# A four-layer convolution and scan kernel: loads in another order, image 0 without the previous image's convolution, setup in two parts, and VectorE in the first and last image

## The chip, the cores and the metric

The kernel runs on one core of a Trainium2 chip. A core has a matrix engine (TensorE; PE in the profile, PEld for its weight loads), a vector engine (VectorE, DVE), an engine for activations (ScalarE, ACT), a general one (GpSimd, POOL), and one that here only issues transfers (SyncE, SP). Each takes its instructions in the order of its own queue and waits on semaphores for the others. Transfers between DRAM and the on-chip memory (SBUF) run on DMA engines beside all this; any of SP and ACT can issue them. The metric is device time in microseconds of one execution, as the median over several.

## The reference

Sixteen images of 192 channels and 32 × 32 pixels (L = 1024) go through four residual layers, each behind a group norm. All is fp32.

```python
x = x + L0(gn(x))   # mLSTM block + silu branch -> 3x3 convolution -> batch norm over all images -> leaky relu
x = x + L1(gn(x))   # channel attention: q, k, v by 1x1 and depthwise 3x3, softmax; project, depthwise, project
x = x + L2(gn(x))   # selective scan in four directions over L: Gelu(depthwise 3x3(in_proj)), project, scan, norm, gate
x = x + L3(gn(x))   # sum of shifted copies (8 shifts in y, 7 in x), weighted by softmax of tanh(products); 1x1, Gelu
```

What matters here: layer 0's batch norm needs statistics of all sixteen images, so everything after it waits for the last image's convolution. L1 and L2 hold ten depthwise 3 × 3 convolutions per image, counted in blocks of 96 or 128 channels: two for v, three for q and k, two for the second one, three in L2. Each output is a sum of nine shifted inputs, each with a factor per channel. L2's recurrence is h[t] = dA[t]·h[t−1] + xt[t].

## The kernel before, in words

Two parts run one after the other.

**Layer 0** is `layer0` (L153). It loads its weights and small vectors, nearly all from the SP queue in the order of the text, and makes two products of weights on PE (`ps<-wg,wT`, `ps<-v_ln_b,w_up` at L39), so that the gates and the norm's offset need no work of their own per image. Then `tc.For_i` at L386 runs over the sixteen images. In pass b a generator `conv3` gives the 3 × 3 convolution of image b − 1, piece by piece: 60 pieces of two matrix passes, in which the function `fill(n)` takes n pieces wherever PE would wait for other engines. Fifteen pieces come before the part of the pass that is written out by hand, two or three each in it. In pass 0 the previous image is taken modulo sixteen, and what is convolved is the padded map `ypad`, which is still zero; what it writes is overwritten by the last convolution, which stands by itself after the loop. Each convolution leaves its result in `ydram` and its statistics in `sdram`.

**Layers 1 to 3** are `LayersB.run` (L860). `setup` (L884) folds the statistics into a scale and an offset (`bsc`, `bsh`), and makes what the layers need: for each depthwise convolution nine diagonal matrices of its factors, made on DVE (L948) and stored to DRAM (`dqd`, `dvd`); the product `w1d` of two weights on PE; the scan's constants (`A`, `dskip`, `xpj`, `sel`), the permutations of L3 (`perm`). All its loads and stores stand in SP's queue, ahead of those of image 0.

Then image by image: `prepare(b)` does L1 and the first half of L2, `scans` the recurrence, `complete(b)` the rest of L2, and L3. These two are generators too; each `yield` names the engine of the next piece. During the scans of image b the pieces of `complete(b-1)` and `prepare(b+1)` are put into gaps by a planner with a cost per instruction and engine clocks of its own (`fits`, `advance`). `prepare(0)` has no scans to lie beside and runs through before them, `complete(15)` after them. In these the order is that of dependences.

In `prepare`, `fill(i, p, pairs)` multiplies by a 1 × 1 weight and copies into a padded map `pad`; `taps` loads the nine diagonals in three thirds into three buffers `dg`; `conv` runs, for each half of the map, nine matrix passes over shifted views of `pad`. The helper's line is L766 in the profile for all engines. At the end a Gelu gives `xg`, which is stored in `xxd` and loaded back by `fetch_xx` into `xx`, since `xx` of the image before may still be read; then the other half of L2's input, z, is made on PE, goes through Gelu on ACT and is stored in `zd`. `begin` starts the first scans: it projects `xx`, makes the steps, stores them (`dld`, `dud`) and loads them back, each row copied to sixteen states (`dl`, `du`).

The scans are 192 units per image, of 128 × 1024 each: ACT makes dA (L1801) and copies du to xt (L1797), DVE multiplies xt by B (L1808) and scans (L1817), POOL multiplies by C (L1829), PE sums over states (L1859). SP loads dl, du and the states in the same order throughout.

In `complete`, each half of the map is loaded from `yd`, normed, gated by z from `zd`, multiplied out and added to x; POOL makes the products. Then fifteen shifted products of x per channel block are made by POOL into a ring of buffers `t`, go through tanh on ACT, and are summed by PE, with symmetric shifts used twice (nine series of two blocks, 34 instructions). The softmax and the weighted sum follow, by blocks, and the last 1 × 1 product `fin`.

Of the kernel before, what the change touches and what calls it, by code (L numbers as in the profile page):

```python
# [20 lines left out]
L = H * W  # L21
HL = L // 2
P6 = 96
# [129 lines left out]
def layer0(tc, cx, NB, ydram, sdram):  # L153
    nc, I = cx.nc, cx.I
    with ExitStack() as ctx:
# [15 lines left out]
        def vec(name, p):  # L171
            v = I[name]
            t = wp.tile([p, v.shape[0] // p], F32, name="v_" + name)
            nc.sync.dma_start(t, v.rearrange("(a p) -> p a", p=p))
            return t
# [5 lines left out]
        w_q = wp.tile([128, 3, INNER], F32, name="w_q")  # L181
        nc.scalar.dma_start(w_q, I["w_q"].rearrange("(k p) o -> p k o", p=128))
        w_k = wp.tile([128, 3, INNER], F32, name="w_k")
        nc.scalar.dma_start(w_k, I["w_k"].rearrange("(k p) o -> p k o", p=128))
# [3 lines left out]
        w_down = wp.tile([128, 3, 256], F32, name="w_down")  # L188
        w_lin = wp.tile([P6, 2, 256], F32, name="w_lin")
        for t, nm, p in ((w_down, "w_down", 128), (w_lin, "w_lin", P6)):  # L190
            nc.sync.dma_start(t[:, :, 0:C], I[nm].rearrange("(k p) o -> p k o", p=p))
            nc.sync.dma_start(t[:, :, C:], I[nm][:, 128:C].rearrange("(k p) o -> p k o", p=p))
        w_c2 = wp.tile([128, 9, C], F32, name="w_c2")
        nc.sync.dma_start(w_c2, I["conv2_wT"][0:128])
        w_c2p = wp.tile([128, 2, 3, C], F32, name="w_c2p")
        for u in range(2):
            r = slice(64 * u, 64 * u + 64)
            taps = I["conv2_wT"][128:C].rearrange("p (y x) o -> p y x o", x=3)
            nc.sync.dma_start(w_c2p[r, 0], taps[:, :, u, :])
            nc.sync.dma_start(w_c2p[r, 1], taps[:, :, 2, :])  # L200
        ln_w, ln_b = vec("ln_w", P6), vec("ln_b", P6)
        b_up = vec("b_up", 128)
        conv_b, skip = vec("conv_b", 128), vec("skip", 128)
        mh_w, mh_b = vec("mh_w", 128), vec("mh_b", 128)

        def vec3(name):
            t = wp.tile([128, 2], F32, name="v_" + name)
            v = I[name].rearrange("(p o) -> p o", o=1)
            nc.sync.dma_start(t[:, 0:1], v[0:128])
            for u in range(2):  # L210
                nc.sync.dma_start(t[64 * u : 64 * u + 64, 1:2], v[128:C])
            return t

        b_down, b_lin, c2_b = vec3("b_down"), vec3("b_lin"), vec3("conv2_b")


        b_if = []
        for nm in ("b_i", "b_f"):
            t = wp.tile([128, 1], F32, name="v_" + nm)
            nc.vector.memset(t, 0.0)  # L220
            for r in range(4):
                for u in range(2):
                    nc.sync.dma_start(
                        t[32 * r + NH * u : 32 * r + NH * u + NH, :], I[nm].rearrange("(h o) -> h o", o=1)
                    )
            b_if.append(t)
        b_i, b_f = b_if
        conv_k = wp.tile([128, 3, 4], F32, name="conv_k")
        nc.sync.dma_start(conv_k, I["conv_k"].rearrange("(k p) t -> p k t", p=128))
        mask = wp.tile([128, 2 * CH], BF16, name="mask")  # L230
        identb = wp.tile([128, 128], BF16, name="identb")
        hmask = wp.tile([128, 4 * HW1], F32, name="hmask")
        nc.sync.dma_start(hmask, I["c_hmask"])
# [8 lines left out]
        for r in range(4):  # L242
            nc.sync.dma_start(sel[32 * r : 32 * r + NH], I["c_sel"])
# [48 lines left out]
        with tc.tile_pool(name="a_pre", bufs=1) as pre:  # L292
            m32 = pre.tile([128, CH], F32, name="m32")
            nc.sync.dma_start(m32, I["c_causal"])
            nc.vector.tensor_copy(
                mask.rearrange("p (i t) -> p i t", i=2),
                m32.unsqueeze(1).to_broadcast([128, 2, CH]),
            )
            wg = pre.tile([128, 9, 2 * NH], F32, name="wg")
            nc.sync.dma_start(wg[:, :, 0:NH], I["w_i"].rearrange("(k p) h -> p k h", p=128))  # L300
            nc.sync.dma_start(wg[:, :, NH:], I["w_f"].rearrange("(k p) h -> p k h", p=128))
            nc.vector.tensor_copy(wg_v[:, :, 0 : 2 * NH], wg[:, 6:9, :])
            for i, nm in enumerate(("w_qT", "w_kT")):
                wT = pre.tile([128, 3, INNER], F32, tag="wT%d" % i, name="wT")
                nc.sync.dma_start(wT, I[nm].rearrange("(k p) o -> p k o", p=128))
                for m in range(3):
                    p = ps()[:, 0 : 2 * NH]
                    matmuls(
                        nc, p,
                        [(wT[:, j, m * 128 : (m + 1) * 128], wg[:, 3 * i + j, :]) for j in range(3)],  # L310
                    )
                    o = wg_qk[:, m, 0 : 2 * NH]
                    if i == 0:
                        nc.vector.tensor_copy(o, p)
                    else:
                        nc.vector.tensor_add(o, o, p)

            p = ps()
            for m in range(6):
                matmuls(  # L320
                    nc, p[:, m : m + 1],
                    [(w_up[:, a, m * 128 : (m + 1) * 128], ln_b[:, a : a + 1]) for a in range(2)],
                )
            nc.vector.tensor_add(b_up, b_up, p[:, 0:6])
            for a in range(2):
                nc.vector.tensor_scalar(
                    w_up[:, a, :], w_up[:, a, :], ln_w[:, a : a + 1], None, op0=ALU.mult
                )

        x_in = wp.tile([128, 3, L + 3], F32, name="x_in")  # L330
# [55 lines left out]
        with tc.For_i(0, NB, 1) as b:  # L386
# [158 lines left out]

            conv = conv3((b + NB - 1) % NB)
# [173 lines left out]

        for _ in conv3(NB - 1):
            pass
# [86 lines left out]
class LayersB:  # L809
# [5 lines left out]
    def __init__(self, tc, cx, NB, ydram, sdram, out):  # L815
        self.tc, self.cx, self.NB = tc, cx, NB
        self.nc, self.I = cx.nc, cx.I
        self.ydram, self.sdram, self.out = ydram, sdram, out
# [35 lines left out]
    def run(self):  # L854
        tc, NB = self.tc, self.NB
        self.bank, self.turn = None, 0
        with ExitStack() as ctx:
# [12 lines left out]
            for _ in self.prepare(0):  # L870
                pass
            self.fetch_xx()
            self.begin()
# [10 lines left out]
    def setup(self):  # L884
        tc, nc, cx, wp, I, NB = self.tc, self.nc, self.cx, self.wp, self.I, self.NB
# [3 lines left out]
        self.w1d = dp.tile([P6, 2, C], F32, name="w1d")  # L889
# [41 lines left out]
        with tc.tile_pool(name="b_pre1", bufs=2) as pre:  # L931
            taps = []
            for m in range(3):
                t = pre.tile([128, 9], F32, tag="tq%d" % m, name="tq")
                with nc.allow_non_contiguous_dma("taps by channel"):
                    nc.sync.dma_start(t, I["dw_qkT"][:, m * 128 : (m + 1) * 128].rearrange("t c -> c t"))
                taps.append((128, t, self.dqd[m]))
            t = pre.tile([128, 3, 9], F32, tag="tw", name="tw")
            nc.sync.dma_start(t, I["dw_w"].rearrange("(g p) t -> p g t", p=128))
            taps += [(128, t[:, g, :], self.dqd[3 + g]) for g in range(3)]  # L940
            for i, nm in enumerate(("dw_v", "dw_kv")):
                t = pre.tile([P6, 2, 9], F32, tag="tv%d" % i, name="tv")
                nc.sync.dma_start(t, I[nm].rearrange("(a p) t -> p a t", p=P6))
                for a in range(2):
                    taps.append((P6, t[:, a, :], self.dvd[i, a]))
            for n, t, dst in taps:
                d = pre.tile([n, 9, n], F32, tag="diag", name="diag")
                nc.vector.tensor_mul(  # L948
                    d, cx.ident[0:n, 0:n].unsqueeze(1).to_broadcast([n, 9, n]),
                    t.unsqueeze(2).to_broadcast([n, 9, n]),  # L950
                )
                nc.sync.dma_start(dst, d)
            wpj = pre.tile([P6, 2, C], F32, tag="wpj", name="wpj")
            nc.sync.dma_start(wpj, I["w_proj"].rearrange("(a p) o -> p a o", p=P6))
            wkv = pre.tile([P6, 2, C], F32, tag="wkv", name="wkv")
            nc.sync.dma_start(wkv, I["w_kvT"].rearrange("(a p) o -> p a o", p=P6))
            w1 = pre.tile([P6, 2, C], F32, tag="w1", name="w1")
            for a in range(2):
                p = self.mm()[0:P6, 0:C]
                matmuls(nc, p, [(wpj[:, i, a * P6 : (a + 1) * P6], wkv[:, i, :]) for i in range(2)])  # L960
                nc.vector.tensor_copy(w1[:, a, :], p)
            nc.sync.dma_start(self.w1d, w1)
# [1005 lines left out]
```

## Time and profile before

The time is 15763.65 us, the median of three executions (15760.87 to 15764.36). The profiled execution took 15761.82 us, and its span, from the first to the last instruction, is 15760.0 us.

| part of the span | us |
|---|---|
| startup, to the loop over images | 0 to 58 |
| sixteen images of layer 0, 201.6 us each | 58 to 3282 |
| last convolution alone | 3282 to 3328 |
| setup, and the load and norm of image 0 | 3328 to 3388 |
| `prepare(0)` | 3388 to 3628 |
| projection and steps for the first scans | 3628 to 3668 |
| scans of sixteen images | 3668 to 15583 |
| `complete(15)` | 15583 to 15760 |

In the whole span PE is busy 80%, DVE 78%, POOL 63%, ACT 59%; DMA moves 154 GB/s on average. These are means over stages with different limits. A row of the trace gives start, length, engine, line, operation, what is written and read, shape and count; in brackets stands how long the engine had been idle before it, and whose work ended that.

### The profile page before, as it was taken

The numbers are of one execution on the slowest core, as the hardware profiler recorded it, in microseconds if no ns is written. First come the engines' busy times: TensorE is split into PE (matmuls) and PEld (weight loads), VectorE is DVE, ScalarE is ACT, GpSimd is POOL, SyncE is SP. The second block draws the span as 40 slices with busy tenths as digits, with TensorE's granted clock in tenths as the row PEclk, the third lists the DMA queues.
The fourth block names the chain that finished last, engine by engine and source line by source line (L and its number), as shares of the span: only waits on it lengthen the run. The fifth ranks groups of instructions, "written<-read, shape, count | busy, mean of one in ns | idle before, by whom it ended". The sixth has DMA issues, their size and how long they took to land. (4 is left out here: it accounts for less than half of the span.)

```text
span 15760.0 us, 197355 instructions
## 1 busy us (share of the span) xinstructions
PE 12662.9 (80%) x72684; PEld 5062.6 (32%) x72684; DVE 12218.0 (78%) x10138; ACT 9273.8 (59%) x12098; POOL 9921.9 (63%) x5837
## 2 busy tenths in 40 slices
PE   8999999987777878778777777777787777878755
PEld 4555555542222222222222222222222222222212
DVE  4444444416898989989888898988989898988995
ACT  3333333325666666666666666666666666666664
POOL 0000000005687878787878787878878787878886
PEclk9999999998787878878788888888888887878766
DMA  1000000016787877778787878787877777777774
GB/s 26 15 15 15 15 14 15 15 47 168 193 202 196 198 199 192 207 185 209 180 209 182 210 186 209 185 210 186 204 193 196 194 200 192 198 201 188 203 181 114
DMA packets 858797, 2421.52 MB, mean 154 GB/s; under 512 B 117952, under 2 KB 237840, under 8 KB 850192
## 3 DMA queue, kind: packets, MB, share of 16 engines
q1 hardware_dynamic: 848592, 2407.09, 59.7%
q8 instruction: 583, 9.55, 0.3%
q10 hardware_dynamic: 9280, 2.08, 0.1%
q14 instruction: 342, 2.80, 0.1%
HBM read 2025.36 MB, written 366.67 MB: 152 GB/s over the span
## 5 line engine op out<-in xcount | busy, mean ns | idle before, releaser
L1829 POOL TENSOR_TENSOR hc<-h,cb 128x1024 f32<-128x1024 f32 x3072 | 7245.4, 2371 | 2057.6 <-DVE h L1817 1546.5
L1817 DVE TENSOR_TENSOR_SCAN h<-dA,xt 128x1024 f32<-128x1024 f32 x3072 | 6914.9, 2273 | 303.6 <-POOL hc L1829 295.9
L1808 DVE TENSOR_TENSOR xt<-xt,bb 128x1024 f32<-128x1024 f32 x3072 | 3632.9, 1227 | 929.7 <-ACT xt L1797 800.6
L1801 ACT ACTIVATE dA<-dl,A 128x1024 f32<-128x1024 f32 x3072 | 3506.3, 1146 | 778.6 <-DMA dl<-dld 670.2
L1859 PE MATMUL acc<-hc,sel 128*32 128x256 f32 x24576 | 2399.7, 471 | 1756.8 <-POOL hc L1829 1753.8
L766 PE MATMUL mm<-pad,dg 96*96 96x512 f32 (+1 forms) x5760 | 2964.3, 650 | 14.4 <-ACT pad L766 11.0
L1797 ACT COPY xt<-du 128x1024 f32<-128x1024 f32 x1536 | 1557.7, 1014 | 1387.9 <-DVE h L1817 1216.3
L1859 PEld LDWEIGHTS acc<-hc,sel 128*32 128x32 f32 x24576 | 560.6, 120 | 4094.9 <-POOL hc L1829 2956.9
L766 PEld LDWEIGHTS mm<-pad,dg 96*96 96x96 f32 (+1 forms) x5760 | 1022.0, 191 | 1517.1 <-issue 1400.8
L583 POOL TENSOR_TENSOR vw<-va,gtok 128x396 f32<-128x396 f32 x112 | 95.3, 851 | 1707.1 <-ACT va L575 1707.1
L766 PE MATMUL mm<-x,wgt 96*128 96x512 f32 (+1 forms) x1664 | 1055.2, 770 | 114.9 <-ACT z L766 42.8
L766 POOL TENSOR_TENSOR t<-x 96x512 f32<-96x512 f32 (+7 forms) x544 | 689.6, 1290 | 212.5 <-PE mm L766 199.9
L1850 PE MATMUL acc<-y,ident 128*128 128x512 f32 x576 | 444.1, 863 | 452.1 <-ACT y L1869 451.4
L678 POOL TENSOR_TENSOR x_in<-x_in,sz 128x384 f32<-128x384 f32 x128 | 116.8, 913 | 749.8 <-DVE x_in L674 674.0
L766 POOL TENSOR_TENSOR dlh<-dlh,e 128x512 f32<-128x512 f32 x384 | 488.6, 1272 | 157.4 <-ACT e L766 151.4
L766 PE MATMUL mm<-d,xT 128*96 128x256 f32 x2048 | 562.3, 412 | 19.2 <-ACT o L766 17.4
L766 POOL TENSOR_TENSOR duh<-dlh,xx 128x512 f32<-128x512 f32 x384 | 537.4, 1399 | 30.2
L766 PE MATMUL mm<-xd,dtw 12*128 12x512 f32 x768 | 532.8, 779 | 14.1 <-ACT dlh L766 14.1
L766 PEld LDWEIGHTS mm<-x,wgt 96*128 96x128 f32 (+1 forms) x1664 | 338.1, 223 | 633.5 <-issue 360.9
L374 PE MATMUL pc<-ypad,w_c 128*128 128x512 f32 (+1 forms) x1224 | 468.3, 631 | 89.3 <-PEq L386 46.1
L609 DVE TENSOR_TENSOR D<-D,s 128x256 f32<-128x256 f32 x768 | 271.0, 415 | 325.9 <-ACT D L606 325.9
L606 ACT ACTIVATE D<-s 128x256 f32<-128x256 f32 x768 | 232.7, 390 | 430.6 <-PE s L600 430.6
(314 smaller groups left out, 15277.6 us busy)
## 6 DMA issues: line engine op xcount, KB each, us to landing
dl<-dld SPq DMA_DIRECT2D x1536, 512.0 KB
du<-dud SPq DMA_DIRECT2D x1536, 512.0 KB
dld<-dlh SPq DMA_DIRECT2D x384, 256.0 KB
dud<-duh SPq DMA_DIRECT2D x384, 256.0 KB
bb<-xdr SPq DMA_DIRECT2D x128, 512.0 KB
cb<-xdr SPq DMA_DIRECT2D x128, 512.0 KB
dg<-dqd SPq DMA_DIRECT2D x288, 192.0 KB
xxd<-xg SPq DMA_DIRECT2D x16, 1536.0 KB
```

Of the source, the lines that this page charges most:

```text
L374: nc.tensor.matmul(p[r, :], lhsT=w_, rhs=v, start=(n == 0), stop=(n == 14))
L606: nc.scalar.activation(d, S[j][:, two], AF.Exp)
L609: nc.vector.tensor_mul(d, d, S[j][:, 2 * CH :])
L678: nc.gpsimd.tensor_mul(hT[:, :, cs], hT[:, :, cs], sz[:, :, cs])
L766: return f(out, *args, **kw)
L1797: self.nc.scalar.copy(self.xt[n], self.du[n])
L1801: self.nc.scalar.activation(self.dA[u % 3], self.dl[n % 2], AF.Exp, scale=self.A[:, blk, n : n + 1])
L1808: self.nc.vector.tensor_mul(self.xt[(n + 1 + blk) % 2], self.xt[n % 2], self.bb[blk])
L1817: nc.vector.tensor_tensor_scan(*views, 0.0, op0=ALU.mult, op1=ALU.add)
L1829: self.nc.gpsimd.tensor_mul(*views)
L1850: nc.tensor.matmul(acc, lhsT=self.cx.ident, rhs=self.y[:, g, half(pair)], start=True, stop=False)
L1859: nc.tensor.matmul(self.acc[rows4(q), q4(s)], lhsT=self.sel[:, m, :], rhs=self.hc[u % 3][:, q4(q)], start=False, stop=(s + m + blk == 3),)
```

## The change

**Startup.** The weights that the two products need (`w_qT`, `w_kT`, `w_i`, `w_f`, `w_up`) are loaded ahead of those that the loop needs (`w_q`, `w_k`, `w_down`, `w_lin`, `w_c2`, `w_c2p`); the loads are shared between SP's queue and ACT's. The product `w1d` of setup is made here. The pool of the temporary tiles is closed after it, and the loop's weights are loaded then.

**Image 0.** The body of the loop becomes a function `image(b, conv)`. Image 0 is called with an empty iterator in place of the convolution, and the loop runs from 1 to 15.

**Setup.** It is cut in two: `setup` keeps what `prepare(0)` needs, `setup_scans` the rest, and is called after twenty pieces of `prepare(0)`. The diagonals are no longer made in `setup`. In image 0, `taps` loads the nine factors per channel (`tv`), DVE makes the diagonals right in `dg`, and SP stores them from there for the later images. `conv` in image 0 gives PE only the first half of the map; the second is made by DVE, with one `tensor_scalar` and eight `scalar_tensor_tensor` on shifted views of `pad`.

**End of `prepare(0)`.** Gelu writes to `xx` itself, with no store and load; `begin` comes ahead of the pieces of z.

**Last image.** `complete(15)` loads y by channel group into `xx` and z into `dA`, both at its beginning, instead of by halves; its products are made by DVE in place of POOL. As a result, the first loads of y lie inside the last image's scans.

```diff
         nc.scalar.dma_start(w_up, I["w_up"].rearrange("(a p) o -> p a o", p=P6))
-        w_q = wp.tile([128, 3, INNER], F32, name="w_q")
-        nc.scalar.dma_start(w_q, I["w_q"].rearrange("(k p) o -> p k o", p=128))
...
+        for i, nm in enumerate(("w_qT", "w_kT")):
+            wTs.append(prp.tile([128, 3, INNER], F32, tag="wT%d" % i, name="wT"))
+            nc.scalar.dma_start(wTs[i], I[nm].rearrange("(k p) o -> p k o", p=128))
...
+        nc.scalar.dma_start(w1d, w1)
+        pre.close()
+
+        w_q = wp.tile([128, 3, INNER], F32, name="w_q")
+        nc.sync.dma_start(w_q, I["w_q"].rearrange("(k p) o -> p k o", p=128))
...
-        with tc.For_i(0, NB, 1) as b:
+        def image(b, conv):
...
-            conv = conv3((b + NB - 1) % NB)
...
+        image(0, iter(()))
+        with tc.For_i(1, NB, 1) as b:
+            image(b, conv3(b - 1))
...
-            for _ in self.prepare(0):
+            first = self.prepare(0)
+            for _ in range(20):
+                next(first)
+            self.setup_scans()
+            while not self.parked:
+                next(first)
+            self.begin()
+            for _ in first:
                 pass
-            self.fetch_xx()
-            self.begin()
...
+    def taps(self, p, src, w, first):
         d = [self.slot("dg", [p, 3, p], "dg", 3) for _ in range(3)]
+        tv = None
+        if first:
+            tv = self.sm.tile([p, 9], F32, tag="tv", name="tv")
+            self.nc.sync.dma_start(tv, w)
         for t in range(3):
+            three = slice(3 * t, 3 * t + 3)
+            if first:
+                self.nc.vector.tensor_mul(
+                    d[t], self.cx.ident[0:p, 0:p].unsqueeze(1).to_broadcast([p, 3, p]),
+                    tv[:, three].unsqueeze(2).to_broadcast([p, 3, p]),
+                )
+                self.nc.sync.dma_start(src[:, three, :], d[t])
+            else:
+                self.nc.sync.dma_start(d[t], src[:, three, :])
+        return d, tv
...
+    def conv(self, out, i, p, taps):
         for hf in range(2):
+            if hf and tv is not None:
+                yield "DVE", 0
+                o = rows(out[:, half(hf)])
+                for t in range(9):
+                    v = self.pads[i][0:p, 16 + t // 3 : 32 + t // 3, t % 3 : t % 3 + W]
+                    if t == 0:
+                        nc.vector.tensor_scalar(o, v, tv[:, 0:1], None, op0=ALU.mult)
+                    else:
+                        nc.vector.scalar_tensor_tensor(
+                            o, v, tv[:, t : t + 1], o, op0=ALU.mult, op1=ALU.add
+                        )
+                continue
...
+        xx = xg if b else self.xx
         for g in range(3):
-            nc.scalar.activation(xg[:, g, :], xg[:, g, :], AF.Gelu, bias=self.dw2b[:, g : g + 1])
+            nc.scalar.activation(xx[:, g, :], xg[:, g, :], AF.Gelu, bias=self.dw2b[:, g : g + 1])
...
+        products = nc.vector if last else nc.gpsimd
+        if last:
+            for g in range(3):
+                nc.sync.dma_start(self.dA[g], self.zd[b, g])
+                nc.sync.dma_start(self.xx[:, g, :], self.yd[g])
...
-                    nc.gpsimd.tensor_mul(t[:, o:], xa[:, o:], xa[:, : L - o])
-                    nc.gpsimd.tensor_mul(t[:, :o], xa[:, :o], xa[:, L - o :])
+                    products.tensor_mul(t[:, o:], xa[:, o:], xa[:, : L - o])
+                    products.tensor_mul(t[:, :o], xa[:, :o], xa[:, L - o :])
```

## The prediction

> **What bounds the kernel now.** I read the busy time by stretch first, with borders that I set where the trace changes character: startup, image loop, last convolution, setup, first image's preparation, its projection, scans, and the last image's end in three pieces. Columns are length, busy time of PE, PEld, DVE, ACT and POOL with counts, the granted TensorE clock, DMA share, GB/s.
>
> ```profile
> 0.00:58.00 58.00, 12.80 (x60) 12.80 (x61) 7.33 (x41) 1.28 (x1) 6.00 (x11) 1.00 0.46 108
> 58.00:3282.00 3224.00, 3104.27 (x28977) 1689.50 (x28977) 1420.86 (x2849) 1249.30 (x2383) 290.90 (x480) 0.99 0.05 14
> ...
> 3328.00:3388.00 60.00, 4.15 (x13) 3.23 (x14) 25.45 (x60) 13.65 (x20) 6.70 (x4) 0.53 0.62 153
> 3388.00:3628.00 240.00, 228.72 (x582) 100.78 (x581) 9.27 (x24) 50.97 (x89) 0.21 (x1) 0.96 0.16 47
> ...
> 3668.00:15583.00 11915.00, 9151.28 (x42504) 3186.22 (x42504) 10739.57 (x7134) 7877.75 (x9500) 9526.45 (x5244) 0.80 0.77 196
> ```
>
> Scans are three quarters of the span and the change leaves them alone. It works in the other stretches: in startup and setup no engine is busy, so something is waited for; preparation is PE alone (228.72 of 240) with DVE idle. Then I read single instructions in order of time, with the wait ahead of each in brackets.
>
> ```profile
> 45.20 4.04 PE L39 MATMUL ps<-wg,wT 128*128 128x24 f32 x18 [45.20 <-DMA wT<-in_w_qT]
> ...
> 3365.30 0.33 SPq L1119 DMA_DIRECT2D x<-in_x  x1
> ...
> 3373.00 1.24 ACT L766 ACTIVATE y<-y,bsh,bsc 96x1024 f32<-96x1024 f32 x1 [7.02 <-DMA y<-ydram]
> ...
> 3431.39 15.62 PE L766 MATMUL mm<-pad,dg 128*128 128x512 f32 x36
> ...
> 3632.93 8.00 PE L766 MATMUL mm<-xx,xpj 128*108 128x512 f32 x12 [4.83 <-DMA xx<-xxd]
> ...
> 15592.03 4.36 PE L766 MATMUL mm<-yh,on 128*128 128x512 f32 x6 [9.79 <-DMA yh<-yd]
> ...
> 15649.39 42.47 POOL L766 TENSOR_TENSOR t<-x 96x1024 f32<-96x1024 f32 x34 [12.50 <-ACT x L766]
> ```
>
> PE does nothing until a weight lands at 45.20; image 0 of the second part starts when its own load, issued at 3365.30 behind some 50 others, has landed; each depthwise convolution costs PE 15.62; a round trip through DRAM, then a POOL series, set the end.
>
> **Startup, about −31.** The transposed weights and gates go ahead of w_q, w_k and the convolution weights. Some 2.7 MB stand up to and including them; DMA moved 237 to 361 GB/s between 3 and 17 us of the trace, so at 270 they take 10 us and land at 13 to 15. Then PE works 4.04 + 5.26 + 4.01 = 13.3 as now, and 2.85 more for the product of w_proj and w_kvT that setup makes now: 14 + 16.2 = 30 for the first group matmul (L91), which is at 61.83 now. Behind that product stand w_q, w_k, w_down and the rest, on SP after its small loads and after a free completion slot; w_q is needed only about 40 us after the group matmul, so this is covered unless SP is over 20 us late. Range −22 to −33.
>
> Here a rule speaks against the change: the Trainium skill ("DMA: Bandwidth & Descriptors", Issuing engines are not separate DMA queues) says that DMAs of all queues share the same 16 engines and that a second issuing engine saves only issue time, usually small. Were it small, all 6.28 MB of the first 60 us would have landed by 6.28/270 = 23 us, and reordering would be worth 8. The trace disagrees: from 20 to 34 us almost nothing moves (0 to 33 GB/s), as SP issues small loads one behind another. I take the trace: −31.
>
> **No convolution in image 0, about −20.** Its 120 matmul passes take about 43 us of PE, on an empty map. But many fill waits. Those between 58 and 80 (14.9 us) stand in the norms' waits for DVE and ACT: worth 1.3 to 3. In the written-out schedule from 141.6 to 242 it is 28.3: five groups of about 2.6 and eight of 1.9. Next to each stand ACT and DVE steps of 1.2 to 1.4 per chunk that PE waits for anyway, so I take 1.7 and 1.0 of each: 16.5. One loop edge goes (46.1 us idle ahead of L374 over 15 edges, 3.1), but image 0 must drain into the loop: 0 to 3. Ends 10 and 43; −20, near the low end because the schedule puts these pieces into waits.
>
> **Setup in two parts, about −27.** About 14 loads stand before x instead of 50, so x is issued when the norm's coefficients are there, near 3337.5, not 3365.30: −27.8. DVE's small constants of the second part (dskip, bn3) now fall between the norm's steps: +0.7. The diagonals go to the convolutions.
>
> **Preparation of image 0, about −87.** PE keeps one half of each of ten convolutions, 18 passes = 7.72; DVE makes the other while PE works. DVE's price: one scaling and eight multiply-adds of 512. The multiply-add in the trace is
>
> ```profile
> L422 DVE SCALAR_TENSOR_TENSOR xact<-x_in,conv_k,xact 128x1024 f32<-128x1024 f32 x144 | 177.5, 1278 | 0.6
> L418 DVE TENSOR_SCALAR xact<-x_in,conv_k 128x1024 f32<-128x1024 f32 x48 | 34.6, 748 | 0.6
> ```
>
> and TENSOR_TENSOR takes 658 for 512 against 1218 for 1024, so 512 less costs 560: 1278 − 560 = 0.72, and about 0.45 for the scaling: 0.45 + 8 × 0.72 = 6.2, plus three diagonal thirds (0.4 to 0.5) of the next: 7.6. PE's own share per convolution is fill 3.43 + 7.72 = 11.1, so DVE fits. By convolution: two of v 2 × 7.72 = 15.4; three of q/k 3 × 7.72 less about 0.7 each, because PE takes the transposes of DVE's half first: 21; two kv, which stand back to back, 31.07 to about 16.4: 14.7; three of the last projection 23.2 less 0.6: 22.6. Sum 73.7. The Gelu writes xx itself, no store and load: PE starts the projection at 3632.93 now, and Gelu ended at 3619.6: −13.2. That is 86.9.
>
> A second rule is against this. The Trainium skill ("Vector Engine (DVE) Microarchitecture Reference", Points that are easy to get wrong) has it that a multiply-add of that form with two SBUF sources that aren't bf16 runs at half throughput. By that each would cost 0.72 + 0.53 = 1.25, DVE's half 10.5 and 11.8 with diagonals: longer than PE's 11.1; each q/k convolution would wait about 2.8 more, the kv pair 7, the last projection about 5 in all; −24 of the gain is lost (total 176). L422 has exactly two fp32 SBUF sources and its 1278 is 60 ns over the plain product's 1218. I take L422.
>
> **Projection to scans, +1.5 (−6 to +6).** The z work used to be hidden in the round trip: three Gelus with two table loads (1.28) each and six copies (0.54). It now stands on ACT between the first decays, and behind ACT wait the copies xt for DVE (L1808): about 3. SP's z stores and the next image's loads wait in order for those Gelus, with the first dl and du loads near them. Against it PE comes to the projection without a pause (its 12 passes take 0.67 each there, 0.43 in the convolutions): −2; and du is issued ahead of a store: −2 or so.
>
> **Inside the scans, +2 (0 to 6).** The order on all engines is the same in all 3072 units. Only in the last image SP takes two loads xx<-yd that must wait for the store of yd to land (3 to 5 us each); dl and du loads stand behind them, and their two-deep rings cover most of it.
>
> **Tail, about −40 (30 to 45).** Now two halves run one after the other: load, means, product, with POOL products 1.24 each (3.71 for three), from 15587.78 to x added at 15642.4. After, y and z are already there except for the last group; the first subtraction is at about 15592.9 instead of 15596.4, the second half needs no load (15615.09 to PE at 15619.40 now) and overlaps; 2 × 6 products at 0.66 instead of 1.24 save the rest: −20. Then 18 rolled products: 16 in two pieces, DVE 1218 plus 98 for the second, 2 at 1.22: 23.5, against 42.47 on POOL: −19. ACT's tanh, 1.06 each, and PE's sums, 1.08 at a clock of 0.50, run beside it and are next in line: they would set 19 to 20. Two adds at the end: −1.2.
>
> **Sum.** −31 −20 −27 −87 +1.5 +2 −40 = −201.5, say −200. The profiled execution took 15761.82 with a span of 15760.0; the span becomes 15560 and its execution 15562. The median is 1.8 above that execution: 15563.6, say 15563.
>
> **Rivals.** (1) DVE doesn't hide: pad reads, diagonals and slots stand one behind another on it, PE waits 2.5 more for each convolution: 25 less, 15588. For: DVE takes diagonals in order and each must wait for PE to leave its slot. Against: 7.6 of 11.1. (2) Given back in the queue: SP's in-order stores and waits late at the start of the scans and in the last image cost 15, w_q comes 15 late in startup, less in between: 15600. For: ACT waits 667.3 us for dl and DVE 800.6 for xt in the scans, so no slack. Against: rings. (3) More: most of image 0's 43 us goes, PE stays at full clock in projection: 15535. (4) The change does nothing that can be measured: the waits it removes are only moved to the next load. Against: PE's 73.7 us cannot return as a load. (5) Slower: landing of dl worsens in all units, because buffers in DRAM and on chip are laid out anew. It needs (200 + 31)/3072 = 0.075 us per unit, a third of the 0.217 that ACT waits for dl now; at 0.09 the time is 15840. Against: same loads in the same order, and h takes 2239 to 2290 ns whatever its buffer.
>
> **Chances.** Differences under 0.2% (31.5 us) can't be told from none here. Forecast as summed 0.58; (1) 0.14; (2) 0.12; (3) 0.11; (4) 0.02; (5) 0.03. So faster 0.95, same 0.02, slower 0.03. The range: parts' ends (22–33, 10–43, ±1, 60–95, ±6, 0–6, 30–45) combined as independent give 15540 to 15600 or so; to take in (1), (2) and (3) it is 15525 to 15625.
>
> **What would show it.** First matmul near 14 and first group matmul near 30; first image's pass 20 shorter than the 201.6 of others; y's ACTIVATE 8 us after the coefficients; 18 passes per convolution with DVE multiply-adds of 0.72 beside; no xxd for image 0; scans again 11915 long; DVE rolls near 24. Wrong if DVE's multiply-adds take over 1 us, if the scan stretch moves by over 15, or if PE still waits for a weight at 40.

## The result, and the profile after

The changed kernel takes 15604.58 us, the median of four executions (15591.93 to 15608.56), against 15764.01 (15760.87 to 15766.58) for the kernel before on the same chip: 0.9897 of the time, with an interval of 0.9886 to 0.9909. That is 159.4 us less, where 200 were forecast. The profiled execution took 15591.93 us and its span is 15590.1, 169.9 below the span of before.

First the busy time of two stretches of the kernel after, with borders at the same events as before (columns: length; busy time and count of PE, PEld, DVE, ACT, POOL; granted clock, DMA share, GB/s): the sixteen images of layer 0, and the first image's preparation.

```profile
29.00:3283.00 3254.00, 3111.09 (x28865) 1693.29 (x28865) 1419.54 (x2847) 1248.00 (x2380) 290.84 (x480) 0.98 0.05 14
...
3341.00:3495.00 154.00, 124.34 (x340) 57.39 (x341) 76.62 (x145) 42.23 (x77) 4.86 (x3) 0.87 0.25 68
```

The images begin at 29 instead of 58, and the preparation is now shared by PE and DVE. The images' granted clock has gone from 0.99 to 0.98, which looks like nothing and is not. Then single instructions of the kernel after in order of time, the counterparts of those shown of before.

```profile
16.25 7.88 PE L39 MATMUL ps<-wg,wT 128*128 128x24 f32 x36 [16.25 <-DMA wg<-in_w_i]
...
31.72 0.37 PE L91 MATMUL ps<-gn_mv,blk 96*96 96x2 f32 x2
...
3336.56 0.36 SPq L1139 DMA_DIRECT2D x<-in_x  x1
...
3386.83 7.89 PE L782 MATMUL mm<-pad,dg 128*128 128x512 f32 x18
...
3388.22 2.33 DVE L782 SCALAR_TENSOR_TENSOR qk<-pad,tv,qk 128x512 f32<-128x512 f32 x3
...
3513.30 5.31 PE L782 MATMUL mm<-xx,xpj 128*108 128x512 f32 x12
...
15501.67 3.56 DVE L782 TENSOR_TENSOR t<-x 96x1024 f32<-96x1024 f32 x4 [4.32 <-ACT x L782]
15506.42 18.84 DVE L782 TENSOR_TENSOR t<-x 96x896 f32<-96x896 f32 x30 [1.18 <-PE mm L782]
```

Each line has moved as the prediction said: PE starts at 16 (14 forecast), x is issued at 3336.56, a convolution is 18 passes beside DVE's multiply-adds, the projection follows without a pause, the rolled products end at 15525.3. So I laid the two traces side by side, cut at events that both have (first group matmul of each image at L91, first 1 × 1 product of the preparation, projection, first xt of the scans, start of the last scan):

| stretch | before | after | difference | forecast |
|---|---|---|---|---|
| to the first group matmul | 61.83 | 31.72 | −30.1 | −31 |
| image 0 | 201.80 | 182.75 | −19.1 | −20 |
| 14 passes of the loop, images 1 to 14 | 2821.78 | 2867.42 | **+45.6** | **0** |
| image 15 and the last convolution | 241.75 | 244.31 | +2.6 | 0 |
| setup, load and norm | 60.51 | 32.67 | −27.8 | −27 |
| `prepare(0)` | 245.27 | 154.43 | −90.8 | −87 |
| projection, first steps | 34.58 | 29.62 | −5.0 | +1.5 |
| scans | 11908.68 | 11906.01 | −2.7 | +2 |
| `complete(15)` | 183.85 | 141.21 | −42.6 | −40 |
| span | 15760.0 | 15590.1 | −169.9 | −201.5 |

One row stands at nothing in the forecast's sum. The loop's body is the same code; its instructions stand in the same order on every engine in both kernels; and yet a pass takes 3.3 us more. A pass of before, from the windows view:

```profile
1272.92:1474.32 201.40, 193.87 (x1813) 105.49 (x1812) 88.80 (x178) 78.16 (x149) 18.17 (x30) 0.99 0.05 14
```

and one of after:

```profile
2055.06:2262.55 207.49, 199.39 (x1812) 108.28 (x1811) 88.90 (x178) 78.36 (x149) 18.18 (x30) 0.96 0.05 14
```

DVE, ACT and POOL work exactly as long; PE is busy 5.5 us longer with the same matmuls, and the clock is lower. Thirteen passes of before last 201.35 to 201.43 (one 203.81); those of after lie anywhere from 201.75 to 207.49.

### The profile page after: what moved, and what is told of

The parts are those of the page before. It is cut to its first block, busy times and chain, and to the rows that moved or that the text cites. A ratio compares the mean times of both kernels' runs of the same rounds, so it can differ in the third digit from the quotient of the medians.

```text
span 15590.1 us, 196674 instructions
## 1 busy us (share of the span) xinstructions
PE 12621.5 (81%) x72384; PEld 5045.6 (32%) x72384; DVE 12310.8 (79%) x10295; ACT 9263.9 (59%) x12084; POOL 9861.8 (63%) x5787
## 5 line engine op out<-in xcount | busy, mean ns | idle before, releaser
L782 PE MATMUL mm<-pad,dg 128*128 128x512 f32 (+1 forms) x5580 | 2899.3, 655 | 13.3 <-ACT pad L782 9.9
L782 PEld LDWEIGHTS mm<-pad,dg 128*128 128x128 f32 (+1 forms) x5580 | 995.5, 192 | 1479.2 <-issue 1363.3
L782 POOL TENSOR_TENSOR t<-x 96x768 f32<-96x768 f32 (+4 forms) x510 | 647.5, 1290 | 204.6 <-PE mm L782 204.2
L782 POOL TENSOR_TENSOR duh<-dlh,xx 128x512 f32<-128x512 f32 x384 | 537.5, 1400 | 30.1
L389 PE MATMUL pc<-ypad,w_c 128*64 128x512 f32 (+1 forms) x1152 | 442.9, 633 | 80.4 <-PEq L735 41.3
```

The costliest lines, as they stand in the source:

```text
L389: nc.tensor.matmul(p[r, :], lhsT=w_, rhs=v, start=(n == 0), stop=(n == 14))
L782: return f(out, *args, **kw)
```

## The experiments

Three explanations stood at the start: that a loop over images 1 to 15 behind a copy of its body is slower in itself (A), that it is chance how the passes fall on a grid on which the clock is decided (B), or that the other parts of the change do it, with weights in other places and another order of loads (C).

### Part by part

`e1_b_alone` is the kernel before with image 0 taken out of the loop and nothing else.

```diff
-        with tc.For_i(0, NB, 1) as b:
+        def image(b, conv):
...
-            conv = conv3((b + NB - 1) % NB)
...
+        image(0, iter(()))
+        with tc.For_i(1, NB, 1) as b:
+            image(b, conv3(b - 1))
```

> The kernel before with one part of the change alone: image 0 without convolution, ahead of a loop over images 1 to 15. Theory A (something in the form of the loop, entered after an image outside it, makes its passes longer): passes of about 205 us instead of 201.4, so 20 gained in image 0 and 47 lost in the loop, some 27 slower than before, near 15791. Theory B (the clock gate is decided on a fixed grid of 3.41 us, and where a pass falls on it depends on all that ran ahead of the loop): passes of either length; at 201.4 the time is 20 shorter, near 15744. Rival C (the load order or the queue ACT of the change disturbs the loop, not this part): passes of 201.4, near 15744, each time.

`e2_b_undone` is the kernel after with image 0 back in the loop.

```diff
-        image(0, iter(()))
-        with tc.For_i(1, NB, 1) as b:
-            image(b, conv3(b - 1))
+        with tc.For_i(0, NB, 1) as b:
+            image(b, conv3((b + NB - 1) % NB))
```

> The changed kernel with this part alone undone: all sixteen images in the loop, image 0 convolving the empty map. Theory A: passes of 201.4, so 47 less in the loop and 20 more in image 0 than the changed kernel, near 15567 against a span of 15590 profiled, and faster than the changed kernel. Theory B: passes of either length. Rival C: passes stay at 205, near 15612.

`e3_unrolled_conv` keeps image 0 outside, and gives it the empty convolution again.

```diff
-        image(0, iter(()))
+        image(0, conv3(NB - 1))
```

> The changed kernel, image 0 still outside the loop, but with the convolution of the empty map in it: tells the place of image 0 from the missing work. Theory A, that the place matters: passes of 205, near 15612. Theory A', that the missing cover of PE matters: passes of 201.4, near 15565. Theory B: either.

`c_after_again` is the changed kernel as it is, on the same chip as these three.

> The changed kernel again, unchanged, for a second trace. Theory A: passes average 205 again with two or three half-clock windows in each, 15592 to 15609. Theory B: another position on the grid, and passes that differ from the first trace pass by pass, on average perhaps 201.4, near 15545.

| kernel | time, us | ratio to before | image 0 | 14 passes |
|---|---|---|---|---|
| e1_b_alone | 15812.87 | 1.0035 [1.0027, 1.0043] | 186.49 | 2882.73 |
| e2_b_undone | 15564.99 | 0.9871 [0.9851, 0.9891] | 199.35 | 2800.96 |
| e3_unrolled_conv | 15610.18 | 0.9901 [0.9882, 0.9921] | 207.92 | 2832.82 |
| c_after_again | 15597.07 | 0.9898 [0.9877, 0.9918] | 183.28 | 2864.05 |

Before took 15754.31 there. With image 0 in the loop the kernel after is 32 us faster than without: a part that saves 19 in its own place costs more than that elsewhere. (20.8 of the 32 belong to e2 itself, as shown below; 11 remain.) Alone (e1) it makes the kernel slower, but for a reason of e1's own. And the third row speaks against "a loop behind a copy is slower": the copy is there, and most passes last 201.2 to 201.9 again. All that e3 changes for the loop is how many instructions PE has had before it.

e1's loss turned out to have a cause of its own, and must not be added to the evidence. In it the instructions of the loop do stand in another order: a piece of convolution that covered PE's wait for DVE has moved. Single instructions of PE in the kernel before:

```profile
1352.63 1.12 PE L374 MATMUL pc<-ypad,w_c2p 64*128 64x512 f32 x2
1353.80 0.27 PE L595 MATMUL s<-mask,identb 128*128 128x256 bf16 x1
```

and the same place in e1_b_alone,

```profile
532.00 0.37 PE L594 MATMUL s<-mask,identb 128*128 128x256 bf16 x1 [2.30 <-DVE qs L536]
```

This wait adds up to 34.0 us in the loop of e1. It was 12.8 us in the loop of before, and behind it e1 runs 107 us more at half clock in the 14 passes (160.4 against 53.4), which is 53.5 lost: 21 + 53.5 = 74.5, where 61 were measured, so that some of it comes back elsewhere. e2 has the same kind of blemish: its pieces at the end of a pass stand otherwise, and its 14 passes are 20.8 shorter than those of before.

### What the loop waits for

Next I asked the waits. PE's and ACT's waits inside the loop, 13 or 14 passes, in the kernel before (columns: line and what it waited for; us in total, times, longest):

```profile
PE ps L39 <- POOL x_in L678: 11.7, 14, 0.9
...
ACT L711 <- DMA sdram<-st: 24.4, 14, 1.8
```

and after:

```profile
PE ps L39 <- POOL x_in L691: 23.5, 13, 1.9
...
ACT L724 <- DMA sdram<-st: 37.2, 13, 3.2
```

Two waits have grown, by 1.0 and 1.1 us per pass (11.7/14 to 23.5/13, 24.4/14 to 37.2/13), and the second causes the first. Each pass ends with three tiny stores of the convolution's statistics, issued from ACT's queue. Here is the end of a pass of the kernel before, ACT, POOL and PE in order of time:

```profile
1248.72 0.37 ACTq L382 DMA_DIRECT2D sdram<-st  x1
1250.30 0.52 ACTq L384 DMA_DIRECT2D sdram<-st  x1
1250.85 1.28 ACT L711 ACT_TABLE_LOAD   x1 [1.74 <-DMA sdram<-st]
...
1260.06 0.91 POOL L678 TENSOR_TENSOR x_in<-x_in,sz 128x384 f32<-128x384 f32 x1 [11.34 <-DVE x_in L674]
...
1261.02 1.56 PE L39 MATMUL ps<-x_in,w_down 128*128 128x512 f32 x3 [0.82 <-POOL x_in L678]
```

and the same in c_after_again:

```profile
594.95 0.39 ACTq L397 DMA_DIRECT2D sdram<-st  x1
597.63 0.51 ACTq L399 DMA_DIRECT2D sdram<-st  x1
598.18 1.28 ACT L724 ACT_TABLE_LOAD   x1 [2.71 <-DMA sdram<-st]
...
607.38 0.90 POOL L691 TENSOR_TENSOR x_in<-x_in,sz 128x384 f32<-128x384 f32 x1 [12.32 <-DVE x_in L687]
...
608.34 4.11 PE L39 MATMUL ps<-x_in,w_down 128*128 128x512 f32 x5 [1.79 <-POOL x_in L691]
```

The second store waits for the first to land: 1.58 before, 2.68 after. ACT stands meanwhile, and behind it stand its own last steps, DVE's x_in, POOL's, and PE's last products. POOL's x_in begins 11.34 behind the first store before and 12.43 here; between x_in and PE nothing has changed. (After the second store ACT loads a table for 1.28 us in any case, so a later landing of that one hardly shows.)

Why does a tiny store land 1.1 later? The DMA records of c_after_again around 595 show it, in my own reading of the packets:

```
595.25 to 596.41   queue 8 "instruction", one packet of 16384 bytes, 1164 ns
595.84 to 596.05   120 of the 128 packets of the store, 48 bytes each
596.40 to 596.52   the other eight, a sixteenth of them
```

Queue 8 carries PE's program: behind layer 0 a median of 256 recorded instructions of PE lies between one such packet and the next, and a pass of some 3640 takes fifteen. In the loops each takes 0.9 to 1.5 us (a few up to 1.9), and I read the trace so that it holds one of the sixteen DMA engines for that time, with the store's packets on that engine behind it. They start half a microsecond late; another 0.6 passes between the last of them and the second store than in the kernel before (1.1 against 0.5), for which the records show no reason. The boundaries fall at the same place in each pass, because the code of the loop is the same each time, and they move when the number of PE instructions ahead of the loop changes. Image 0 emitted once more ahead of the loop has moved them. The fetch nearest to the first store, by kernel (negative: ahead of it):

| kernel | fetch starts, us after the first store | first store to second, us | mean pass |
|---|---|---|---|
| before | −3.2 | 1.57 to 1.61 | 201.6 |
| after | +0.3 to +0.9 | 2.50 to 3.14 | 204.8 |
| e3_unrolled_conv | +1.2 to +1.6 | 1.57, twice 3.3 to 3.5 | 202.3 |

The two passes of e3 in which the first store was hit took 207.2 and 204.6. This gave a theory that can be tried: shift the boundaries, or take ACT out of the wait.

### Moving the fetch, and moving the stores

`e5_after_shift` is the kernel after with 34 matmuls of one column each at the very beginning, while PE waits for its first weights anyway.

```diff
+        with tc.tile_pool(name="a_idle", bufs=1, space=PSUM) as idle:
+            p = idle.tile([32, 1], F32, name="idle")
+            for _ in range(34):
+                nc.tensor.matmul(p, lhsT=cx.ones[:, 0:32], rhs=cx.ones[:, 0:1], start=True, stop=True)
```

> The changed kernel with 34 small matrix products into an unused PSUM tile put ahead of everything on PE, in its wait for the first weights; all engines' order in the loop stays as it was. They only move the loop's place in PE's instruction stream, by 136 of the 256 instructions that one fetch of 16 KB holds. Theory D (a fetch of PE's instructions, which in the changed kernel starts 0.3 to 0.9 us after each first store of statistics, holds one DMA engine for about 1.1 us; the store lands late, ACT waits for it, PE's wait at the end of the pass grows from 0.8 to 1.8, and the clock gate grants half the clock in one window more): the fetch moves to about 3.5 us ahead of the store, the store's wait returns to 1.6, passes to 201 to 202, 40 to 47 gained in the loop, near 15560. Theory B (chance position on the clock's grid): passes stay anywhere between 201 and 208, with no tie to the store. Rival E (the loop behind an image outside it is slower by its form): passes stay at 205, time near 15600.

`e6_before_shift` is the kernel before with the same lines.

> The kernel before, with the same 34 products ahead of everything and nothing else changed. Theory D: the next fetch after the one 3.2 us ahead of the store comes 3.6 us later, so about 0.4 after the store; its wait grows from 1.6 to 2.5 to 3.2, and passes become 204 to 206: 45 to 65 slower than before. Theory B and rival E: passes stay at 201.4 and the time is that of before.

`e4_stats_sp` is the kernel after with the stores on SP's queue, which computes nothing.

```diff
-            nc.scalar.dma_start(stats(slice(0, 128)), st[:, 0:2, :].rearrange("p h s -> p (h s)"))
+            nc.sync.dma_start(stats(slice(0, 128)), st[:, 0:2, :].rearrange("p h s -> p (h s)"))
             for hf, r in enumerate((lower, upper)):
-                nc.scalar.dma_start(stats(slice(128, C))[:, 6 * hf : 6 * hf + 6], st[r, 2, :])
+                nc.sync.dma_start(stats(slice(128, C))[:, 6 * hf : 6 * hf + 6], st[r, 2, :])
```

> The changed kernel with the three stores of statistics of each image issued from SP instead of ACT. Theory D: ACT no longer waits for them to land, PE's wait at the end of the pass is 0.9 or less wherever the fetch falls, and the passes take 201.5 or less, so the time is about 45 less than the changed kernel's, near 15555; faster than both kernels. Theory B: passes vary as before with the grid. Rival E: 205, no gain.

`e8_before_shift14`, made after these, is the kernel before with 14 such matmuls, chosen so that the fetch falls where it falls in the kernel after.

> The kernel before with 14 of the small products ahead of everything on PE in place of 34, and nothing else. In the changed kernel the first fetch of a pass starts at its 202nd PE instruction and the one that hits the store at 3529 to 3533 (the store is issued when PE is at 3527); in the kernel before they are at 259 and 3414, and with 34 products (136 instructions) at 127 and 3504. So 14 products (56 instructions) should put the first at about 203 and copy the changed kernel's places. Theory D: the fetch falls 0.3 to 0.9 us after the store, the store's wait grows from 1.6 to 2.5 to 3.2, passes become 204 to 206, and the time is 40 to 65 above the kernel before's. Theory B (chance) and rival E (form of the loop): passes of 201.4, time as before.

| kernel | time, us | ratio to before | fetch after the first store | first store to second | 14 passes | at half clock in them |
|---|---|---|---|---|---|---|
| e5_after_shift | 15554.53 | 0.9865 [0.9848, 0.9881] | −2.8 | 1.56 to 1.67 | 2817.68 | 47.2 |
| e4_stats_sp | 15548.52 | 0.9871 [0.9853, 0.9890] | −3.2 to −2.8 | 1.89 to 2.12 | 2817.46 | 87.8 |
| e6_before_shift | 15779.78 | 1.0004 [0.9996, 1.0013] | −1.7 | 1.58 | 2822.10 | 53.8 |
| e8_before_shift14 | 15793.43 | 1.0022 [1.0014, 1.0031] | +0.85 to +1.67 | 1.58, or 3.05 to 3.77 | 2840.04 | 75.1 |

Thirty-four idle matmuls give the loop its old length back: 2817.68 against 2867.42, with the first group matmul at 31.03 (31.72 without them). The instructions of a pass stand in the same order on every engine as in the kernel after. The waits of e5 in the loop:

```profile
PE ps L39 <- POOL x_in L695: 8.9, 13, 0.8
...
ACT L728 <- DMA sdram<-st: 20.8, 13, 1.7
```

e6 missed: its fetch was expected 0.4 behind the store and came 1.7 before it, so nothing was hit and nothing was lost. The place had been worked out by counting instructions, and the count was off. e8 came nearer. Its fetch falls between the two stores and hits the first in some passes only, so that one kernel holds both cases: of the 14 passes, the four with a hit took 202.65, 204.90, 207.39 and 202.81; those without 201.28 to 201.61 seven times, and 204.14 to 204.15 three times, each of these the first or second behind a hit. The kernel before can thus be given the loss of the kernel after by matmuls that compute nothing, in the passes where the fetch meets the store.

The packets say the same over all kernels that store from ACT's queue. In 68 passes eight packets of the first store start behind the end of the fetch, and the second store comes 2.46 to 3.77 us after the first; in the other 102 none does, and it comes 1.44 to 1.67 after.

e4 takes the wait away from ACT. It is, at 15548.52, faster than both kernels; e5, at 15554.53, can't be told from it. Measured each against before on its own chip, they gain some 40 to 50 us on the kernel after. But e4 is no clean trial of the wait. With the stores gone, ACT's steps of the loop stand in another order, with 5 table loads per pass in place of 9, so that ACT is busy 5.1 us less; a piece of convolution has moved on PE too; and its stores are issued about 3 us behind the fetch, so no fetch met one. What shows the cause is e5, and e8 by its passes.

### Why 1 us costs 3.3

The wait grew by 1 us, the pass by 3.3. The rest is the clock. In the kernel after, the windows of a slow pass behind its two last waits:

```profile
2250.40:2253.85 3.45, 3.45 (x5) 1.35 (x4) 1.33 (x2) 0.69 (x1) 0.00 (x0) 0.51 0.02 5
...
2260.60:2264.10 3.50, 3.45 (x7) 1.32 (x6) 2.40 (x10) 0.27 (x1) 0.00 (x0) 0.51 0.00 0
```

and PE's instructions there:

```profile
2249.63 7.11 PE L39 MATMUL ps<-x_in,w_down 128*128 128x512 f32 x12 [1.73 <-POOL x_in L691]
2259.69 0.69 PE L389 MATMUL pc<-ypad,w_c 128*128 128x512 f32 x1 [2.94 <-PEq L735]
```

All changes of the granted clock in one execution stand on one grid of 3.413 us. The Trainium skill ("TensorE: Matmul & The Clock Gate", Part 1) says that the clock falls to half after an idle window of about 3.4 us. The trace agrees on the length and on the half (0.51), but PE need not be idle for the whole window. I counted PE's idle time per window of the grid in the 14 passes of all twelve traces:

| PE idle in a window of 3.413 us | windows | the next at half clock |
|---|---|---|
| under 1.4 us | 9662 | 97, of these 46 behind another at half clock |
| 1.4 to 1.6 us | 83 | 2 |
| over 1.6 us | 225 | 212 |

About half a window is enough. Before, the wait of 0.82 stayed below; after, 1.8 is on the edge. Of its 14 waits, 11 lie with 1.60 to 1.86 us in one window (here, 1.73 of 2246.98 to 2250.39), and the next runs at half clock, which costs 1.7 us; the other three have 1.11 to 1.60 in one window, and nothing follows. In the 14 passes after, 118.0 us run at half clock, against 47.2 in e5: (118.0 − 47.2)/2 = 35.4, and PE's wait for x_in in them is 15.6 longer: 51.0. Measured are 2867.42 − 2817.68 = 49.7.

The passes of before are even on this grid: 201.38 is 59 × 3.4133, and the half-clock window at the loop's edge comes 197.8 us behind the first group matmul of each. The last nine passes of e4 are so too, with two half-clock windows in the same places in each, as this one, from the windows view of e4_stats_sp:

```profile
1421.36:1622.77 201.41, 195.04 (x1813) 106.84 (x1813) 88.75 (x178) 73.02 (x145) 18.18 (x30) 0.98 0.05 14
```

What holds a loop to the grid isn't shown: e5 also has one half-clock window at the edge in nearly every pass, and its passes take 200.79 to 201.36 (one 202.77).

### Two terms of the forecast by themselves

`e7_pe_both` is the kernel after with both halves of image 0's convolutions on PE.

```diff
-            if hf and tv is not None:
+            if hf and tv is None and False:
```

> The changed kernel, with PE making both halves of image 0's ten depthwise convolutions (DVE still makes the diagonals). My sum had 73.7 us for DVE's halves: the preparation of image 0 goes from 154.4 to 228. If DVE's multiply-adds ran at half throughput, DVE's share would be worth about 50 and the preparation would go to 205. The rest of the kernel is as in the changed one, its loop perhaps near 205 per pass.

It took 15698.03 us in its one execution, and `prepare(0)` in it 228.71 against 154.43. DVE's share is worth 74.3, give or take 5: the same code of `prepare(0)` took 153.8 to 159.3 in seven traces. A convolution is again, in single instructions of e7_pe_both,

```profile
3393.59 15.62 PE L782 MATMUL mm<-pad,dg 96*96 96x512 f32 x36
```

`e9_one_queue` is the kernel after with all of startup's loads on SP's queue, in the same order of text.

```diff
-        nc.scalar.dma_start(w_up, I["w_up"].rearrange("(a p) o -> p a o", p=P6))
+        nc.sync.dma_start(w_up, I["w_up"].rearrange("(a p) o -> p a o", p=P6))
...
-            nc.scalar.dma_start(wTs[i], I[nm].rearrange("(k p) o -> p k o", p=128))
+            nc.sync.dma_start(wTs[i], I[nm].rearrange("(k p) o -> p k o", p=128))
...
-        nc.scalar.dma_start(wg[:, :, NH:], I["w_f"].rearrange("(k p) h -> p k h", p=128))
+        nc.sync.dma_start(wg[:, :, NH:], I["w_f"].rearrange("(k p) h -> p k h", p=128))
...
-        nc.scalar.dma_start(w1d, w1)
+        nc.sync.dma_start(w1d, w1)
```

> The changed kernel with all loads of its startup on SP's queue, in the same order of the text, so that the order is kept and the sharing with ACT's queue is undone. If the order brought the gain of startup, as the rule has it that a second issuing engine saves only issue time, the first group matmul stays at 31 to 34. If the sharing brought it, because SP stands before small loads, it goes to 40 or later. The loop's order on all engines is that of the changed kernel, and no PE instruction ahead of it changes, so passes of about 205.

It took 15601.44 us in its one execution. Its first instructions of PE:

```profile
15.13 7.85 PE L39 MATMUL ps<-wg,wT 128*128 128x24 f32 x36 [15.13 <-DMA wg<-in_w_f]
...
30.57 0.37 PE L91 MATMUL ps<-gn_mv,blk 96*96 96x2 f32 x2
```

PE starts no later than with two queues (15.37 to 16.25 in six traces). The second queue brought nothing that this shows; of the gain of startup, what the loads gave, they gave by their order.

## Why the prediction was right or wrong

The time lies in the range and the sign is right, but in part by luck: one term was missed by 48.2 us, and the others together gave 16.6 more than forecast, so that the span is 31.6 above the sum (the median 41.6 above the forecast). Where the missed loss is gone, in e5, the time is 15554.53 for the 15563 forecast.

**The step that failed** is "No convolution in image 0, about −20". Its own place gave what was forecast (−19.1), but it counted the work taken out and one loop edge, and took the other fifteen images as they were; what it costs to emit the body once more ahead of the loop was put at "image 0 must drain into the loop: 0 to 3". It cost 45.6 in the 14 passes and 2.6 at image 15. The forecast's own list of signs shows the gap: it asked for image 0 to be 20 shorter than "the 201.6 of others", and none of the three signs of being wrong looked at the others. The 201.35 to 201.43 of the passes before were in the trace, and so were the fetches; nothing in the working asked what else a pass depends on.

**Startup** was right (−30.1), with PE's start at 16.25 and not 14. But some 6 us of it belong to the second term. e2, with the same loads and image 0 in the loop, has four passes of the empty convolution ahead of its first group matmul, and they wait for their weights:

```profile
34.44 3.35 PE L389 MATMUL pc<-ypad,w_c 128*128 128x512 f32 x4 [3.37 <-DMA w_c<-in_conv_wT]
...
37.63 0.25 PE L91 MATMUL ps<-gn_mv,blk 96*96 96x2 f32 x2
```

So the order of the loads gave about 24 (−30.1 + 37.63 − 31.72), and the missing convolution about 25. What was wrong is the weighing of the rule on issuing engines: I set it up as speaking against −31, but it speaks of sharing loads between queues, and there it holds (e9). The 8 us were a wrong use of it.

**Inside image 0** something was not foreseen: the empty convolution had kept PE busy, and without it the clock falls (0.80 granted from 34 to 60 us; 1.00 before, from 62 to 100). The two groups of eight norm products, in the kernel after:

```profile
36.44 6.42 PE L39 MATMUL ps<-xn,on 96*96 96x512 f32 x8 [2.95 <-DVE xn L107]
...
44.72 5.37 PE L39 MATMUL ps<-sq,on 96*96 96x512 f32 x8 [1.87 <-ACT sq L124]
```

Before, they took 3.60 each; 4.6 are lost together, and −19.1 came out with this loss in it.

**Setup** was right: −27.8, x issued at 3336.56 (3337.5 forecast).

**`prepare(0)`**: −90.8 for −87. The group of the kernel after with its mean ns:

```profile
L782 DVE SCALAR_TENSOR_TENSOR qk<-pad,tv,qk 128x512 f32<-128x512 f32 x24 | 18.0, 750 | 0.6
```

0.75 for 0.72; half throughput would have been 1.25 by the forecast's estimate. (The losses that it listed for that case add up to 20.4, not 24.) So the rule on two fp32 sources does not show here, and the choice of the row was right. e7 gives the split: 74.3 for DVE's share (73.7 forecast), and 245.27 − 228.71 = 16.6 for the rest, where the spared store and load were put at 13.2.

**Projection to scans**: −5.0 for +1.5. The 2 us for PE's coming without a pause were right (8.00 to 5.31). The Gelus of z did cost time, but behind the first xt, so that it stands in the row of the scans. They and their table loads lie on ACT between the first decays, and DVE waits for xt:

```profile
3542.90 1.28 ACT L782 ACT_TABLE_LOAD   x1
...
3561.85 2.37 DVE L1842 TENSOR_TENSOR xt<-xt,bb 128x1024 f32<-128x1024 f32 x2 [5.38 <-ACT xt L1831]
```

From ACT's first xt to DVE's ninth scan it is 31.2 us in all four traces with z ahead of the scans, 38.8 in the kernel after, and 36.8 to 41.1 in all eight with z behind. So 7.6 were lost there; with the −5.0 it makes +2.6, near the +1.5 forecast. **Scans**: −2.7 for +2, with these 7.6 in it. The stretch lies anywhere from 11897 to 11947 over the runs of the changed scans, with the same code, so the row can't be told from nothing, and a move of 15 would have shown nothing either. Nor can the last image's scan, where I had put the waits for yd: it is 4.9 longer here (686.9 to 691.8), but 686.9 to 691.1 and 689.6 to 692.2 over the runs of either kind.

**Tail**: −42.6 for −40. DVE's rolled products take 23.6 (23.5 forecast, 42.47 on POOL).

**The rivals.** The measured time is nearest to that of the second, "given back in the queue: 15600", but not by its mechanism: PE waited for no load in image 0, the start of the scans lost 7.6 and not 15, by ACT's Gelus, and e9, with more on SP, loses nothing. A right number for a wrong reason. The first (DVE doesn't hide), the third (image 0 gives most of 43) and the fifth (dl lands later in all units) did not happen.

What is open: in which passes a fetch hits is explained by its place, but I can't compute that place from the code before running (e6 missed by 2.1 us, e8 by ten instructions and more). And 51 of the windows with under 1.4 us of idle time were followed by half clock with no other half-clock window ahead. All 51 hold one place of the pass, where PE waits three times 0.33 us for DVE's qs (0.72 to 1.04 idle in the window), and so do as many windows that nothing followed; why it happens there is open. What the fetch does in stretches other than the loop wasn't tried.

## What to carry to other kernels

When a loop's body is emitted once more ahead of the loop, or code ahead of it is taken out, compare the length of every pass afterwards, not only the part that was changed: the fetch of instructions falls on other places in each pass. A tiny store whose landing a computing engine waits for is the place where this hurts; try to issue it from a queue that computes nothing (here 40 to 50 us of 15600, with fewer table loads as part of it). And when waits on TensorE are counted, ask whether they make up half of a clock window: 1 us more of waiting cost 3.3 here.

## What was not expected of the hardware

- A fetch of PE's instructions, a packet of 16384 bytes that takes 0.9 to 1.5 us, delays a store of 48-byte packets: where eight of its 128 packets come behind the fetch, the next store, which waits for its landing, follows after 2.5 to 3.8 us instead of 1.6.
- On the grid of 3.413 us on which the granted clock changes, a window with over 1.6 us of idle PE was followed by half clock in 212 of 225 cases, with no full window of idle time needed.
- A loop can run in step with this grid: 13 passes of before within 0.1 us of each other at 201.38 = 59 × 3.4133. With the fetch on the store, passes of the same body differ by up to 5.7 (201.75 to 207.49).
- Products on empty data were worth something: without them PE's granted clock was 0.80 in the first norms of image 0.
